# One VectorE instruction for mask and row maximum, a power on GpSimd for a root, and a reordered start, in an attention and feed-forward kernel

## The chip, the cores and the metric

The kernel runs on one core of one Trainium2 chip. Such a core has TensorE (PE; its weight loads are listed apart as PEld), VectorE (DVE), ScalarE (ACT), GpSimd (POOL) and a queue (SP) that issues DMAs between the chip's main memory and SBUF. TensorE writes its products into PSUM. The metric is the device time of one execution in microseconds, as a median over runs. Beside it stands the span of one profiled execution, from its first to its last instruction.

## The reference

One transformer layer in fp32, for x of shape 2 x 1024 x 512, with 16 heads of 32 and a hidden width of 2048:

```python
qkv = einsum('bsd,ed->bse', x, w_qkv) + b_qkv
scores = einsum('bhqd,bhkd->bhqk', q, k) / sqrt(32)
attn = softmax(scores + causal)          # causal: -inf above the diagonal
y = einsum('bsd,ed->bse', attn @ v, w_out) + b_out
x = layernorm(x + y)                     # (x - mean) / sqrt(var + 1e-5)
h = relu(einsum('bsd,hd->bsh', x, sign(up_weight)) * up_scale)
x = layernorm(x + einsum('bsh,dh->bsd', h, sign(down_weight)) * down_scale * output_scale)
```

## The kernel before

**Order.** The kernel does not issue instructions in the order of its loops. Every instruction or small group is given to a planner as a task: the engines that may run it with a cost for each (in microseconds), a due time called place, and the buffers that it reads, writes and updates. `Plan.schedule` then lists the tasks engine by engine: of those whose inputs would be ready by the planner's own clock, the one with the smallest place goes first. The order so found is fixed in the program; on the chip each engine runs its queue in that order and waits on semaphores. A changed cost or place can therefore move instructions anywhere.

**Attention.** The heads are taken in 8 chunks of four heads: 4 chunks for each batch element, in a row. A chunk needs its keys and queries for 1024 tokens (`product`, L549: fp32 matmuls of 128x512, four to a result), split into a high and a low part (ScalarE and VectorE for keys, L626 and L631; VectorE and GpSimd for queries, L570, L609 and L614) and copied by 32 small DMAs per part into "stacks" (`stack`; all DMAs are issued on L505), from which scores are computed at the faster fp32r rate. It also needs values (`values_of`, L586). The projection of the next chunk goes on while the present one attends: a chunk lasts `STEP = 36` units of place, keys and queries are due by `MID` of it (0.55), values from there to `HI` (1.0).

For each block of 128 query tokens, i = 0 to 7, and each head, only the keys up to that block count, so that N = 128 (i + 1) columns. Heads are grouped: four to a score tile for i below 2, two for i = 2 and 3, one above. `scores` does for one such group: the score matmuls into a PSUM pair, of which there are two (L789, or L770 in the first half of the first chunk, from unsplit keys and queries); the mask added to the diagonal block (L805); the row maximum of all its heads in one instruction, negated (L815); for each head the exponential with the maximum as bias and the row sum as a second output (L821); one reciprocal (L832); for each head the scaling of the row on GpSimd (L838). `transposes` turns the rows by TensorE (L859) and copies them out of PSUM (L487 on ScalarE, L489 on VectorE). `values` multiplies with the values (L888), at times for two query blocks together (those in `TOGETHER` are held back for the next), and VectorE adds the bias into atT (L908).

**Output projection and first normalisation.** In the last chunk of a batch element, `output` loads the rows of x, adds b_out on GpSimd (L944), multiplies by w_out (L950), adds (L961) and takes mean and variance (L965, L969). When all eight blocks are done, `normalise` takes the root of eight variances at once on ScalarE (L979), the reciprocal on VectorE (L983), and scales the eight blocks on VectorE (L988).

**Feed-forward.** Four blocks of 512 tokens. `turn` transposes the rows and splits them (L1013, L1020, L1025). For each of 16 hidden slices: eight matmuls (L1062), ReLU on ScalarE into hf (L1073), a split (L1079, L1084), eight matmuls into four PSUM banks pd (L1099). At the end of a block, for each of its four row tiles: scaling by output_scale and down_scale (L1113), the residual (L1123), statistics (L1129, L1134), root (L1139), reciprocal (L1145), scaling (L1150) and the store.

**Start.** `first_half` warms TensorE with 24 transposes (L703), loads the first weights on ScalarE's queue and the first 512 tokens of xT on SP's, four DMAs, computes keys and then queries of those tokens (the scheduler interleaves them), and starts attention with them. `hold` keeps the DMAs of the next tokens and of the value weights behind the landing of the first piece of xT by a one-column copy (L694).

Of the kernel before, what the change touches and what calls it, by code (L numbers as in the profile page):

```python
# [18 lines left out]
P = 128  # L19
EPS = 1e-5  # L20

MASKED = -3.0e38


# [5 lines left out]
LAST = [0, 1, 2, 7, 6, 5, 4, 3]  # L30
HURRY = 6.0

LAG = 6.0

MID, HI = 0.55, 1.0

# [238 lines left out]
def kernel(  # L275
# [26 lines left out]
    NFC = F // P  # L302
    TB = 512
    TPB = TB // P
    NG = F // TB
# [10 lines left out]

    mask = const.tile([P, P], F32, tag="mask", name="mask")
    nc.gpsimd.memset(mask, 0.0)
    nc.gpsimd.affine_select(
        out=mask,  # L320
        in_=mask,
        compare_op=ALU.is_ge,
# [5 lines left out]
    epst = const.tile([P, 1], F32, tag="eps", name="epst")  # L328
    nc.gpsimd.memset(epst, EPS)
    bqk = const.tile([P, b_qkvP.shape[1]], F32, tag="bqk", name="bqk")  # L330
    nc.gpsimd.dma_start(bqk, b_qkvP)
# [30 lines left out]
    def place_for(stack, name, n, kind=F32, side="left"):  # L362
# [14 lines left out]

    a_pr, a_pt = place_for(left, "probs", 4 * 2 * TB), place_for(left, "probsT", 8 * 2 * TB)

# [23 lines left out]
        "raw": [None],  # L403
        "hf": [None] * 4,
        "hh": [None] * 6,
# [14 lines left out]
    def reopen(cls):  # L420

        if cls == "raw" or cls == "xt" and homes["xt"][0] is None:
            right.close()
            xt = place_for(right, "xt0", 2 * NC * TB, F32R, "right")
            homes["xt"][:1] = views(xt, (2, NC, TB), F32R)
            raw = place_for(right, "raw", NC * TB, side="right")
            homes["raw"] = views(raw, (NC, TB))
        elif cls == "pd":
            wide.close()
            narrow = wide.enter_context(tc.tile_pool(name="narrow", bufs=1, space=PSUM))  # L430
            homes["pd"] = [
                narrow.tile([P, TB], F32, tag=f"pd{k}", name=f"pd{k}") for k in range(4)
            ]
        else:
            left.close()
            xt = place_for(left, "xt1", 2 * NC * TB, F32R)
            homes["xt"][1:] = views(xt, (2, NC, TB), F32R)
            homes["hf"] = views(place_for(left, "hf", 4 * TB), (TB,))
            hid = place_for(left, "hid", 12 * TB, F32R)
            homes["hh"] = views(hid, (TB,), F32R)[:6]  # L440
            homes["hr"] = views(hid, (TB,), F32R)[6:]

    def of(t):
# [8 lines left out]
    rings = {  # L452
        "pr": (a_pr, 4 * 2 * TB // P), "pt": (a_pt, 8 * 2 * TB // P)
    }
# [125 lines left out]
    def values_of(b, e, v, t0, place):  # L580

        xt, w, ps = inputs[b], weights[b, e], new("f")
        for t in range(4):
            for c in range(NC):
                def fn(_, t=t, c=c):
                    nc.tensor.matmul(  # L586
                        of(ps)[:, t, :],
                        lhsT=of(xt)[:, c, t0 + t * P : t0 + (t + 1) * P],
                        rhs=of(w)[:, c, 2, :],
                        start=(c == 0),  # L590
                        stop=(c == NC - 1),
                    )

                plan.task(
                    {"PE": (0.218, 0.218)}, fn, place(1), [xt[c, t0], w[2]], updates=[ps[0]],
                    count=2, label="ps_v",
                )

        plan.task(
            copy(TB),  # L600
            lambda g: copied(g, of(v)[:, t0 // P : t0 // P + 4, :], of(ps)),
            place(0) - FAST, [ps[0]], [v[t0]], label="v",
        )
# [94 lines left out]
    def first_half():  # L698
# [9 lines left out]
        for c, z in ((0, 1), (1, NC)):  # L708
# [9 lines left out]
            )  # L718
        load_x(0, -100, [0])
        xt = inputs[0]  # L720
        load_w(0, 0, -95, [0], act_queue)
# [8 lines left out]
        rows = lambda n: of(kq)[:, n * TB : (n + 1) * TB]  # L730
        for n in (1, 0):
            ps = product(0, 0, n, 0, lambda units: -50)
            with_bias(0, 0, n, lambda n=n: rows(n), [kq[n]], ps, -50)
        values_of(0, 0, v, 0, lambda units=0: -1)
        plain[0, 0] = kq, v

    def second_half():
# [3 lines left out]
        place = pace(-10, 6, 16 * 3)  # L741
        split(hl, 0, lambda: of(kq)[:, TB : 2 * TB], [kq[1]], -20)
        stack(st, 1, hl, 0, 0, TB, lambda: -20)
# [17 lines left out]
    def scores(b, e, i, heads, at):  # L761
# [3 lines left out]
        if (b, e) in plain and i < NQ // 2:  # L765
            kq = plain[b, e][0]

            def fn(_):
# [9 lines left out]
            plan.task(  # L778
                {"PE": (0.002 + N / 485,) * 2}, fn, at - EAGER, [kq[0], kq[1]], updates=[sc[0]],
                count=2 * G, label="sc4",  # L780
            )
        else:
            st = made[b, e][0]
            for j, u in enumerate(heads):
                for k0 in range(0, N, TB):
# [15 lines left out]
                    )  # L801
        sc3 = lambda: of(sc).rearrange("p (g w) -> p g w", g=G)
        plan.task(
            dve(0.163 + 0.134 * G),
            lambda _: nc.vector.tensor_tensor(  # L805
                sc3()[:, :, ts(i, P)],
                sc3()[:, :, ts(i, P)],
                mask[:, None, :].to_broadcast([P, G, P]),
                ALU.add,
            ),  # L810
            at, updates=[sc[0]], label="mask",
        )
        plan.task(
            dve(0.15 + 1.046 * N * G / 1000),
            lambda _: nc.vector.tensor_reduce(of(nm)[:, :G], sc3()[:, :, :N], AX.X, ALU.max, negate=True),  # L815
            at, [sc[0]], [nm[0]], label="max",
        )
        for j in range(G):
            plan.task(
                {"ACT": (0.355 + 0.838 * N / 1000, 0.46 + 0.838 * N / 1000)},  # L820
                lambda _, j=j: nc.scalar.activation(  # L821
                    of(pr)[:, j * N : (j + 1) * N],
                    of(sc)[:, j * W : j * W + N],
                    AF.Exp,
                    bias=of(nm)[:, j : j + 1],
                    accum_out=of(sums)[:, j : j + 1],
                ),
                at, [sc[0], nm[0]], [pr[j], sums[0]], label="exp",
            )
# [108 lines left out]
    def output(b, i, place):  # L938

        xb, st, a, py = new("xb"), new("st6"), atT[b, i], new("f")  # L940
        y = x1[b]
        dma(place(), lambda: of(xb), lambda: x[ts(b * NQ + i, P), :], 256, writes=[xb[0]])
        plan.task(
# [29 lines left out]
    def normalise(b, at):  # L973

        y, m = x1[b], mv[b]
        rs = lambda: of(m)[:, :, 2]
        plan.task(
            {"ACT": (2.8, 2.0)},
            lambda _: nc.scalar.activation(rs(), of(m)[:, :, 1], AF.Sqrt, bias=epst),  # L979
            at, [m[0]], [m[1]], label="sqrt",  # L980
        )
        plan.task(
            dve(0.16), lambda _: nc.vector.reciprocal(rs(), rs()), at, updates=[m[1]], label="rs"  # L983
        )
# [58 lines left out]
    def feed_forward(up, dn, dsc, base):  # L1043
        UNIT = 2.0

        def block(tb):
# [61 lines left out]
            for t in range(TPB):  # L1108
# [10 lines left out]
                if not final:  # L1119
# [28 lines left out]
                plan.task(  # L1148
                    {**dve(0.546), **pool(0.69)} if final and t + 1 < TPB else dve(0.546),
                    lambda e, m=m, y=y: engine[e].tensor_scalar(  # L1150
                        of(y), of(y), of(m)[:, 0:1], of(m)[:, 2:3], ALU.subtract, ALU.mult
# [14 lines left out]
    for at, (b, e) in enumerate(chunks):  # L1166
# [7 lines left out]
        for i in tiles:  # L1174
            begin[i] = past
            attend(b, e, i, past, i in TOGETHER and not (at == 0 and i < NQ // 2))
            past += i + 1
# [102 lines left out]
```

## Time and profile before

| | |
|---|---|
| median of three runs | 770.89 us (770.79 to 771.13) |
| the profiled execution: time, span | 772.01 us, 770.2 us |
| TensorE clock granted | 0.997 |
| busy in the span: PE, PEld, DVE, ACT, POOL | 752.4, 571.3, 519.6, 379.4, 257.1 us |
| busy of those before 517 us (attention) | 507.5, 375.9, 400.3, 318.9, 238.6 us |
| mask (L805) and maximum (L815), busy | 62.3 and 180.2 us, 178 instructions each |

An entry such as `L815 DVE TENSOR_REDUCE small<-d` names the line of the kernel, the engine, the operation, and the buffers written and read. The profile's views used here are the page of totals, a table by stretches of time (busy PE, PEld, DVE, ACT, POOL with instruction counts in brackets, then the clock, the DMA engines' share and GB/s), the list of who waited for whom (total us, times, longest), and the timeline (start, duration, instruction, and in square brackets the idle time before it and what ended it). Matmuls are pipelined and their ends are modelled, so that a PE shown busy need not be at full rate.

### The profile page before, as it was taken

How to read it: one execution, taken by the hardware profiler on the slowest of the kernel's cores; microseconds unless marked ns; L12 is line 12 of the kernel's file. 1: busy time of each engine (PE TensorE's matmuls, PEld its weight loads, DVE VectorE, ACT ScalarE, POOL GpSimd, SP SyncE). 2: the span in 40 equal slices, each digit the busy share in tenths (PEclk: the TensorE clock that was granted, in tenths of full speed). 3: DMA queues.
4: the chain of work that ended last, by engine and by line, in shares of the span. 5: the costliest groups of instructions: out<-in, count | busy, mean ns of one | idle time of the engine just before them, and what ended most of it. 6: DMA issues, size and time to landing. Idle time of an engine off the chain costs nothing.

```text
span 770.2 us, 15411 instructions
## 1 busy us (share of the span) xinstructions
PE 752.4 (98%) x5864; PEld 571.3 (74%) x5864; DVE 519.6 (67%) x1087; ACT 379.4 (49%) x841; POOL 257.1 (33%) x325
## 2 busy tenths in 40 slices
PE   8999999999999999899999999999999999999995
PEld 4668769778766775686876887758777887878884
DVE  1658898688787677878778889946336337335535
ACT  1426766776754556577756777744222222222210
POOL 2315455463446443544544644530002002002002
PEclk9999999999999999999999999999999999999998
DMA  6467556058151523532614514433001001000101
GB/s 182 107 156 157 142 111 138 14 116 223 34 124 46 120 69 69 126 82 56 139 27 101 120 57 138 137 110 110 1 0 56 1 0 56 1 0 1 55 0 55
DMA packets 38089, 62.35 MB, mean 81 GB/s; under 512 B 6016, under 2 KB 18304, under 8 KB 38016
## 3 DMA queue, kind: packets, MB, share of 16 engines
q1 hardware_dynamic: 36912, 60.85, 30.8%
q8 instruction: 46, 0.75, 0.4%
q10 hardware_dynamic: 1072, 0.52, 0.2%
q14 instruction: 27, 0.22, 0.1%
q0 software_dynamic: 32, 0.01, 0.0%
HBM read 24.66 MB, written 4.19 MB: 37 GB/s over the span
## 4 chain that ended last, share of the span: by engine, by line
PE 51%; DVE 5%; SPq 1%; ACT 1%; issue 1%; DMA 1%; POOL 0%; POOLq 0%; DVEq 0%; ACTq 0%
PE s L1062 14%; PE pd L1099 14%; PE s L859 6%; PE s L888 4%; PE d L789 4%; PE s L549 3%; PE s L950 3%; PE s L586 2%; SPq L505 1%; DVE small L1129 1%; PE s L1013 1%; DVE x L988 1%; DVE atT L1113 1%; DMA stacks<-wqkv 1%; DVE atT L1150 0%
## 5 line engine op out<-in xcount | busy, mean ns | idle before, releaser
L838 POOL TENSOR_SCALAR probs<-probs,small 128x128 f32<-128x128 f32 (+7 forms) x256 | 188.9, 747 | 243.2 <-DVE small L832 216.2
L821 ACT ACTIVATE probs<-d,small 128x128 f32<-128x128 f32 (+7 forms) x256 | 189.2, 747 | 73.5 <-DVE small L815 37.5
L815 DVE TENSOR_REDUCE small<-d 128x1 f32<-128x768 f32 (+9 forms) x178 | 180.2, 1016 | 3.0
L859 PE MATMUL s<-ident,probs 128*128 128x128 f32 x1152 | 162.7, 273 | 3.1 <-POOL probs L838 1.9
L859 PEld LDWEIGHTS s<-ident,probs 128*128 128x128 f32 x1152 | 134.0, 140 | 42.1 <-issue 20.0
L487 ACT COPY probsT<-s 128x512 f32<-128x512 f32 (+3 forms) x193 | 95.3, 523 | 92.3 <-PE s L859 82.4
L1099 PE MATMUL pd<-stacks,hid 128*128 128x512 f32 x512 | 133.4, 399 | 0.5 <-DVE hid L1079 0.5
L1062 PE MATMUL s<-xt,stacks 128*128 128x512 f32 x512 | 133.2, 400 | 0.0
L549 PE MATMUL s<-xT,wqkv 128*128 128x512 f32 x256 | 128.4, 598 | 1.0 <-DMA wqkv<-in_w_qkvT 1.0
L789 PE MATMUL d<-stacks 128*128 128x512 f32 (+2 forms) x368 | 123.7, 426 | 2.8 <-DMA stacks<-wqkv 1.4
L1073 ACT ACTIVATE hf<-s,ups 128x512 f32<-128x512 f32 x64 | 44.0, 687 | 160.2 <-PE s L1062 158.7
L1099 PEld LDWEIGHTS pd<-stacks,hid 128*128 128x128 f32 x512 | 94.3, 188 | 24.1 <-DVE hid L1079 1.4
L1062 PEld LDWEIGHTS s<-xt,stacks 128*128 128x128 f32 x512 | 94.3, 188 | 23.5 <-issue 1.0
L1079 DVE CAST hid<-hf 128x512 fp32r<-128x512 f32 x64 | 27.7, 435 | 121.6 <-ACT hf L1073 121.5
L489 DVE COPY probsT<-s 128x512 f32<-128x512 f32 (+3 forms) x152 | 86.9, 587 | 17.3 <-PE s L859 11.7
L789 PEld LDWEIGHTS d<-stacks 128*128 128x128 f32 x368 | 59.6, 190 | 39.1 <-issue 24.5
L805 DVE TENSOR_TENSOR d<-d,mask 128x128 f32<-128x128 f32 (+2 forms) x178 | 62.3, 352 | 29.3 <-PE d L789 23.4
L888 PEld LDWEIGHTS s<-probsT,v 128*32 128x32 f32 x2304 | 60.4, 110 | 18.7 <-issue 5.4
L586 PE MATMUL s<-wqkv,xT 128*128 128x128 f32 x512 | 72.9, 276 | 0.0
L888 PE MATMUL s<-probsT,v 128*32 128x128 f32 x2304 | 71.6, 274 | 0.2 <-DVE probsT L489 0.2
L586 PEld LDWEIGHTS s<-wqkv,xT 128*128 128x128 f32 x512 | 66.3, 192 | 6.4 <-issue 5.4
L950 PE MATMUL s<-wout,atT 128*128 128x512 f32 x128 | 64.1, 597 | 0.1
(65 smaller groups left out, 486.9 us busy)
## 6 DMA issues: line engine op xcount, KB each, us to landing
stacks<-wqkv SPq DMA_DIRECT2D x224, 128.0 KB, 2.4
wqkv<-in_w_qkvT SPq DMA_DIRECT2D x22, 256.0 KB, 3.5
xT<-in_xT SPq DMA_DIRECT2D x16, 256.0 KB, 5.3
rows<-in_x SPq DMA_DIRECT2D x16, 256.0 KB, 3.0
raw<-in_up_wT SPq DMA_DIRECT2D x4, 1024.0 KB, 5.0
out<-atT SPq DMA_DIRECT2D x16, 256.0 KB, 2.0
stacks<-wqkv SPq DMA_DIRECT2D x48, 64.0 KB, 2.0
raw<-in_down_wT SPq DMA_DIRECT2D x2, 1024.0 KB, 5.8
```

The lines of the kernel that those rows point to most:

```text
L487: nc.scalar.copy(dst, src)
L549: nc.tensor.matmul(of(ps).rearrange("p a b -> p (a b)"), lhsT=of(w)[:, c, n, :], rhs=of(xt)[:, c, t0 : t0 + TB], start=(c == 0), stop=(c = ...
L586: nc.tensor.matmul(of(ps)[:, t, :], lhsT=of(xt)[:, c, t0 + t * P : t0 + (t + 1) * P], rhs=of(w)[:, c, 2, :], start=(c == 0), stop=(c == NC ...
L789: nc.tensor.matmul(of(sc)[:, j * W + k0 : j * W + k1], lhsT=of(st)[:, 0, u, ts(i, P)], rhs=of(st)[:, 1, u, k0:k1], start=True, stop=True,)
L815: lambda _: nc.vector.tensor_reduce(of(nm)[:, :G], sc3()[:, :, :N], AX.X, ALU.max, negate=True),
L821: lambda _, j=j: nc.scalar.activation(of(pr)[:, j * N : (j + 1) * N], of(sc)[:, j * W : j * W + N], AF.Exp, bias=of(nm)[:, j : j + 1], acc ...
L838: lambda _, j=j: nc.gpsimd.tensor_scalar(of(pr)[:, j * N : (j + 1) * N], of(pr)[:, j * N : (j + 1) * N], of(sums)[:, j : j + 1], 1.0, ALU. ...
L859: lambda _, k=k, c=c, tp=tp: nc.tensor.transpose(of(tp)[:, k, :], of(pr)[:, c], ident),
L888: nc.tensor.matmul(of(to)[ts(u, HD), n, :], lhsT=of(v)[:, k, ts(u, HD)], rhs=of(pt)[:, ts(c + k, P)], start=(k == i), stop=(k == 0),)
L950: lambda _, c=c: nc.tensor.matmul(bank(py), lhsT=of(a)[:, c, :], rhs=of(wout)[:, c, :], start=(c == 0), stop=(c == NC - 1),),
L1062: lambda _, f=f, c=c, n=n, pu=pu: nc.tensor.matmul(of(pu), lhsT=of(up)[:, f // TPB, c, ts(f % TPB, P)], rhs=of(xt)[:, n, c, :], start=(c = ...
L1099: lambda _, f=f, t=t, n=n, h=h: nc.tensor.matmul(of(pds[t]), lhsT=of(h)[:, ts(t, P)], rhs=of(dn)[:, f // 4, f % 4, :], start=(f == 0 and n ...
```

## The change

- **Mask and maximum.** For each head, one two-operand VectorE instruction reads the N score columns and the last N columns of a mask that is now 1024 wide (zeros, with the triangle in the last 128), writes -(score + mask) back over the scores, and gives their minimum, with the largest float as the start value, as a second output. That minimum is the negated maximum. The exponential takes scale -1, and depends on its own head's instruction alone.
- **First normalisation.** The root on ScalarE and the reciprocal on VectorE give way to two GpSimd instructions on eight columns: add epsilon, then raise to the power -0.5.
- **First tokens.** The first 512 tokens of xT are loaded as 256 (four DMAs) and 256 (one DMA), and their keys and queries computed and copied out by halves, in that order; what reads them depends on the half that it needs.
- **Next keys.** `MID` is 0.45 in place of 0.55.
- **Room for the mask.** The ring of transposed rows has 60 blocks of 128 in place of 64, and hf has three buffers in place of four.
- **Small parts.** The planner places the loads of rows in `output` after the last stack DMA known by then. In the last block of the feed-forward the final scaling (L1150) is for VectorE alone; before, GpSimd might take it. The last query block of a chunk is never held back.

```diff
-MID, HI = 0.55, 1.0
+MID, HI = 0.45, 1.0
...
-    mask = const.tile([P, P], F32, tag="mask", name="mask")
+    mask = const.tile([P, S], F32, tag="mask", name="mask")
     nc.gpsimd.memset(mask, 0.0)
     nc.gpsimd.affine_select(
-        out=mask,
-        in_=mask,
+        out=mask[:, S - P :],
+        in_=mask[:, S - P :],
...
-    a_pr, a_pt = place_for(left, "probs", 4 * 2 * TB), place_for(left, "probsT", 8 * 2 * TB)
+    a_pr, a_pt = place_for(left, "probs", 4 * 2 * TB), place_for(left, "probsT", PTB * P)
...
-        "hf": [None] * 4,
+        "hf": [None] * 3,
...
-        load_x(0, -100, [0])
-        xt = inputs[0]
+        xt = inputs[0] = new("xT")
+        for t0, pieces in ((0, NC), (HB, 1)):
+            for c in range(0, NC, NC // pieces):
+                z = c + NC // pieces
+                dma(
+                    -100,
+                    lambda c=c, z=z, t0=t0: of(xt)[:, c:z, t0 : t0 + HB],
...
-        for n in (1, 0):
-            ps = product(0, 0, n, 0, lambda units: -50)
-            with_bias(0, 0, n, lambda n=n: rows(n), [kq[n]], ps, -50)
+        for t0 in (0, HB):
+            for n in (1, 0):
+                ps = new("f")
+                for c in range(NC):
...
+                        nc.tensor.matmul(
+                            bank(ps)[:, :HB],
+                            lhsT=of(w)[:, c, n, :],
+                            rhs=of(xt)[:, c, t0 : t0 + HB],
...
-        plan.task(
-            dve(0.163 + 0.134 * G),
-            lambda _: nc.vector.tensor_tensor(
-                sc3()[:, :, ts(i, P)],
-                sc3()[:, :, ts(i, P)],
-                mask[:, None, :].to_broadcast([P, G, P]),
-                ALU.add,
-            ),
-            at, updates=[sc[0]], label="mask",
-        )
-        plan.task(
-            dve(0.15 + 1.046 * N * G / 1000),
-            lambda _: nc.vector.tensor_reduce(of(nm)[:, :G], sc3()[:, :, :N], AX.X, ALU.max, negate=True),
-            at, [sc[0]], [nm[0]], label="max",
-        )
+        for j in range(G):
+            some = lambda j=j: of(sc)[:, j * W : j * W + N]
+            plan.task(
+                dve(0.17 + 1.046 * N / 1000),
+                lambda _, j=j, some=some: nc.vector.tensor_tensor_reduce(
+                    some(),
+                    some(),
+                    mask[:, S - N :],
+                    scale=-1.0,
+                    scalar=LARGEST,
+                    op0=ALU.add,
+                    op1=ALU.min,
+                    accum_out=of(nm)[:, j : j + 1],
+                ),
+                at, [sc[0]], [sc[1, j], nm[j]], label="max",
+            )
...
                     bias=of(nm)[:, j : j + 1],
+                    scale=-1.0,
                     accum_out=of(sums)[:, j : j + 1],
                 ),
-                at, [sc[0], nm[0]], [pr[j], sums[0]], label="exp",
+                at, [sc[1, j], nm[j]], [pr[j], sums[0]], label="exp",
...
-        dma(place(), lambda: of(xb), lambda: x[ts(b * NQ + i, P), :], 256, writes=[xb[0]])
+        dma(
+            place(), lambda: of(xb), lambda: x[ts(b * NQ + i, P), :], 256, writes=[xb[0]],
+            after=[latest["stack"]],
+        )
...
         plan.task(
-            {"ACT": (2.8, 2.0)},
-            lambda _: nc.scalar.activation(rs(), of(m)[:, :, 1], AF.Sqrt, bias=epst),
-            at, [m[0]], [m[1]], label="sqrt",
+            pool(0.3),
+            lambda _: nc.gpsimd.tensor_scalar(
+                rs(), of(m)[:, :, 1], EPS, 1.0, ALU.add, ALU.mult
+            ),
+            at, [m[0]], [m[1]], label="eps",
         )
         plan.task(
-            dve(0.16), lambda _: nc.vector.reciprocal(rs(), rs()), at, updates=[m[1]], label="rs"
+            pool(1.2),
+            lambda _: nc.gpsimd.tensor_tensor(
+                rs(), rs(), half.to_broadcast([P, NQ]), ALU.pow
+            ),
+            at, updates=[m[1]], label="rs",
         )
...
-                    {**dve(0.546), **pool(0.69)} if final and t + 1 < TPB else dve(0.546),
-                    lambda e, m=m, y=y: engine[e].tensor_scalar(
+                    dve(0.546),
+                    lambda _, m=m, y=y: nc.vector.tensor_scalar(
...
-            attend(b, e, i, past, i in TOGETHER and not (at == 0 and i < NQ // 2))
+            apart = i == tiles[-1] or at == 0 and i < NQ // 2
+            attend(b, e, i, past, i in TOGETHER and not apart)
```

## The prediction

> **What bounds the kernel now.** I read the page's busy times first, then the table of stretches of 20 us, then who the PE waited for, then the timeline around each hole.
>
> ```profile
> span 770.2 us, 15411 instructions
> ...
> PE 752.4 (98%) x5864; PEld 571.3 (74%) x5864; DVE 519.6 (67%) x1087; ACT 379.4 (49%) x841; POOL 257.1 (33%) x325
> ...
> 0.00:20.00 20.00, 16.59 (x60) 9.23 (x60) 3.74 (x14) 3.47 (x10) 5.11 (x16) 1.00 0.60 179
> ...
> 180.00:200.00 20.00, 18.45 (x245) 15.58 (x245) 16.22 (x34) 13.47 (x25) 8.10 (x8) 1.00 0.62 178
> ...
> 300.00:320.00 20.00, 17.70 (x139) 11.51 (x142) 18.73 (x41) 11.57 (x23) 7.08 (x8) 1.00 0.54 120
> ...
> 380.00:400.00 20.00, 18.58 (x239) 16.73 (x238) 14.09 (x28) 14.07 (x39) 7.86 (x12) 1.00 0.36 78
> ```
>
> In the stretches the numbers are PE, PEld, DVE, ACT, POOL busy. TensorE is the bound: it idles only 17.8 us (770.2 - 752.4): 3.4 in the first 20 us, 1.55, 2.30 and 1.42 in the three later stretches, 7.7 after its last matmul, 1.4 scattered. From 517 us on (feed-forward) it is packed. What the change can win lies in the start, three holes, the end, and waits too short to show as idle. The latter are in the waits of the weight loads:
>
> ```profile
> PEld d L789 <- ACT probs L821: 12.7, 37, 1.3
> PEld s L859 <- POOL probs L838: 11.4, 25, 2.0
> ```
>
> A score matmul waits until the exponential has freed its PSUM pair; a transpose waits for a normalised row. Both stand at the end of mask, maximum, exponential, scaling. TensorE feels part of these 24.1 us (62 waits), since it still drains what was issued: its own waits for the exponential are 1.4 us.
>
> **What the Trainium skill says.** "VectorE: DVE Perf Modes", Why PSUM operands drop a tier: an fp32 operand in PSUM holds VectorE to one element a cycle. The trace agrees: maxima of 1024 and 640 columns take 1221 and 819 ns, 1.05 ns an element and 0.15 fixed. The same page, Two Vector instructions with no wait between them: an operation that also gives out its accumulator is two instructions; the changed kernel's VectorE queue shows both, the before trace no VectorE one. "Vector Engine (DVE) Microarchitecture Reference", Points that are easy to get wrong: the two-tensor form with an accumulator runs at half speed when both sources are non-bf16 in SBUF. Here one is in PSUM; L631, of this mix but without an accumulator, shows no halving (741 ns for 512 columns). "GPSIMD Engine Reference", Key points: GpSimd shares its SBUF interfaces with VectorE, to the cost of two-port instructions there. The trace agrees:
>
> ```profile
> 306.65 0.55 DVE L988 TENSOR_SCALAR x<-x,small 128x512 f32<-128x512 f32 x1
> ...
> 310.79 3.65 DVE L988 TENSOR_SCALAR x<-x,small 128x512 f32<-128x512 f32 x4
> ```
>
> The first had POOL idle (0.55 us); the four stood beside POOL work and took 0.91 each.
>
> **The change, part by part.**
>
> *Mask and maximum.* Removed: L805 and L815, 62.3 + 180.2 = 242.5 us in 356 instructions. Added: 256 pairs, one per head and row tile. Columns: 8 chunks x 4 heads x 128 x (1+...+8) = 147,456, by 1.05 ns 155 us; fixed 0.15 (maximum) to 0.20 (L631), 45 us; the read-out by VectorE's smallest instructions (four in 0.33 us) 0.08, 20 us. Sum 220: VectorE gets 22 us back. Bounds: 40 us back (read-out free, 0.15 fixed), or, at half speed, 310 + 71 = 381, 139 us more. I take 220, as L631's mix is the nearest. More important is the delay to the exponential. One head of 1024 columns: mask start to maximum end was 1.54 us (190.70 to 192.24), now 1.02 x 1.05 + 0.2 + 0.1 = 1.38. Two heads of 384: 1.43 before both; now 0.7 for the first. Four of 256: 1.9; now 0.55. Taking 0.15 from each of the 62 waits gives 9.3 us of weight-load waiting; TensorE sees less than half. I book -3.5 (0 to -9).
>
> *Keys at 0.45.* One hole is keys' and queries' stacks landing late: at 389.03 a score matmul had waited 1.42 us for stacks<-wqkv. SP issued the last 18 of 32 stack DMAs from 368.48 to 386.24, each queued behind the landing of an earlier one. In the built order, summing TensorE work by the trace's intervals, the last key/query product stands 12.6 us ahead of that chunk in before, 15.1 in after: about the 2.5 needed. In the first batch it stands 15 to 17 ahead; 1 to 3 in before are early products of the chunk after. The values are spread up to and past each chunk's start. At 190.47 to 192.02 TensorE had neither values nor products left (next batch's xT still loading) and waited 1.55 for POOL's rows; in after 12 value products stand there. I book -1.4 and -1.5 (0 to -3 together; up to +3 if the later-freed xT delays the second batch's loads: these eight are queued on SP behind one more 256 KB rows load).
>
> *First normalisation.* On ACT two table loads of 1.28 and a root of 0.31 sat at 301.55 to 307.26 around a copy, and the exponential whose maximum was ready at 304.25 began at 307.28; then TensorE waited 0.45 for it. This goes. The eight L988 remain bunched ahead of the next fused instructions, and held two score tiles (0.94 and 0.91 of TensorE idle). The power is on GpSimd: no row of before has one. Lower bound: a short POOL instruction, 0.37 (128 columns); upper 5 us, an estimate of over ten times that[...]. Behind it on POOL stand a row scaling and a split, behind the first L988 on VectorE a bias, copies and the next maxima. I take 1 us: -1.0 of the 2.3 (to +3 at 5 us). The second normalisation lies in the packed feed-forward: nothing, covered by its matmuls until those tokens' transposes, some 60 us later (L988 near 528, L1013 of xT from 590).
>
> *Start.* Before: the first product ran 5.9 to 7.8, TensorE waited for query weights until 8.81, then 6 x 0.857 to 14.23, and 0.94 for the bias copies. Now two half products precede the same wait; the weights come on ACT's own queue, behind the same bytes: 8.7 again. Then 6 x 0.43, 0.6 bias, 0.5 scores, second halves 8 x 0.43: at 15.8 TensorE has done what before had done at 15.67. Of before's gaps until 32 us (six of about 0.2) about 0.8 close, as the first softmax starts 3 us earlier: -0.7 (+1 to -2). The mask's fill is 8 times wider (0.20 now; at POOL's 0.84 ns a column up to 0.95) and holds back the identity, warm-up and the bias load by 0.75: covered by the weights' wait; uncovered, it costs that. The extra half-width DMA is one SP issue of 0.45, in the shadow of the first loads.
>
> *End.* From 762.46 VectorE was continuous until its last instruction:
>
> ```profile
> 762.51 0.74 DVE L1113 SCALAR_TENSOR_TENSOR atT<-pd,osc,v 128x512 f32<-128x512 f32 x1
> ...
> 763.42 2.07 POOL L1150 TENSOR_SCALAR atT<-atT,small 128x512 f32<-128x512 f32 x1 [0.69 <-DVE small L1145]
> 763.83 0.90 DVE L1123 TENSOR_TENSOR atT<-atT,xT 128x512 f32<-128x512 f32 x1
> ...
> 766.30 0.55 DVE L1150 TENSOR_SCALAR atT<-atT,small 128x512 f32<-128x512 f32 x1
> ```
>
> Two final scalings move from POOL (2.07 each) to VectorE (0.52); in the built order the second falls after the last matmul, +0.52; the add at 763.83 had been slowed from 0.69 to 0.90 by POOL and gets 0.2 back; one add moves to POOL, off the end. +0.4 (0 to +0.7).
>
> *At nothing:* three buffers for four behind ReLU (one is used every 3.7 us, free after about 2), ring of 60 blocks for 64 (44 held plus two units of 7 fit either; a wrap may cost a short wait), the later-ordered rows loads (POOL waited 15 us for these with TensorE running). The condition on the last tile names no tile of TOGETHER.
>
> *Sum:* -3.5 - 2.9 - 1.0 - 0.7 + 0.4 = -7.7. A new order moves about 5000 TensorE instructions, and its own short waits can't be read from the trace: I give back 2, an estimate from holes of 1.4 to 2.3 that the old order left. -5.7: span 764.5. The profiled execution took 772.0, 1.1 above the median of 770.89 and 1.8 above its span; against the median 765.2.
>
> **Rivals.**
> *Forecast, 0.50:* half the short waits and most holes close: 762 to 768.5.
> *Short waits vanish too, 0.13:* the 62 waits were mostly felt, and the order is kept: 5 us more, 760. For: TensorE's busy time contains modelled ends. Against: only 1.4 of the 12.7 shows as its own wait.
> *Gain lost in the order, 0.27:* each hole was filled by earlier products, which then lack elsewhere; late xT or a slow power opens another. Then 768 to 777, most likely 770.5, that is unchanged. For: no work is removed from TensorE (same matmuls, 8 split in two). Against: the holes have distinct causes, and each is addressed.
> *VectorE becomes the bound, 0.10, slower:* the fused instruction runs at half speed. 139 us more on the 400 that VectorE has before 517 us gives 539; in its fullest stretch it reached 94% with TensorE losing 2.3 of 20, so 539/0.94 = 573, 56 later: 827. It decides from about 1.2 ns an element, where 147,456 x 1.2 + 66 fixed equals the 242.5 removed. For: no accumulator on VectorE in the trace. Against: L631.
>
> **How the numbers follow.** Measurement tells 0.2% (1.5 us). Faster: 0.50 + 0.13 + 0.06 of the third = 0.69; same 0.10; slower 0.11 + 0.10. Range 759.5 to 773 takes in the forecast, most of the second, two thirds of the third; the forecast's own is 762 to 768.5.
>
> **What would show it.** Fused rows near 1.3 us at 1024 columns with a read-out under 0.2; VectorE under 505 us in all; weight-load waits for exponentials and rows well under 24; no idle for stacks; no table load before the feed-forward; first scores near 12.2 (15.17 before); TensorE's last matmul at 754 to 759 and the end some 8.1 after it. Wrong if fused rows exceed 1.45, the power exceeds 3, or new holes over 1 us open where the second batch's xT arrives.

## The result and the profile after

The changed kernel takes 776.18 us (median of 6 runs, 775.27 to 776.88) beside 771.01 us for the kernel before (6 runs, 770.14 to 771.34): ratio 1.0068, 95% interval 1.0055 to 1.0081. It is 5.2 us slower, where 5.7 us faster was forecast. The page of the changed kernel:

```profile
span 774.1 us, 15524 instructions
...
PE 756.1 (98%) x5880; PEld 574.9 (74%) x5880; DVE 492.4 (64%) x1258; ACT 368.9 (48%) x823; POOL 259.1 (33%) x329
```

VectorE has 27.2 us less to do (519.6 before). TensorE, with the same products, shows 3.7 us *more* busy time and the same idle (18.0 us for 17.8). The ends of matmuls are modelled, so a matmul whose successor comes a little late may look longer: a loss that shows as busy time is likely to be many short delays, with few holes. The stretches, first of the changed kernel (columns as in the prediction: PE, PEld, DVE, ACT, POOL busy, then clock, DMA share, GB/s):

```profile
0.00:20.00 20.00, 17.12 (x81) 12.85 (x82) 5.17 (x27) 5.66 (x19) 6.76 (x19) 1.00 0.54 161
...
140.00:160.00 20.00, 19.32 (x186) 14.21 (x185) 15.69 (x50) 14.60 (x47) 10.15 (x18) 1.00 0.05 15
180.00:200.00 20.00, 20.00 (x276) 18.85 (x276) 14.70 (x43) 12.67 (x31) 10.01 (x11) 1.00 0.68 167
200.00:220.00 20.00, 18.91 (x168) 12.50 (x167) 15.91 (x48) 13.81 (x39) 10.01 (x18) 1.00 0.31 93
300.00:320.00 20.00, 19.77 (x147) 13.15 (x146) 17.71 (x42) 11.44 (x24) 11.33 (x13) 1.00 0.50 110
340.00:360.00 20.00, 19.31 (x172) 13.15 (x171) 15.59 (x47) 14.28 (x40) 10.73 (x19) 1.00 0.05 14
```

And three of the kernel before:

```profile
140.00:160.00 20.00, 20.00 (x177) 13.56 (x176) 15.57 (x30) 14.86 (x42) 7.79 (x14) 1.00 0.14 31
...
200.00:220.00 20.00, 20.00 (x178) 13.74 (x176) 15.78 (x33) 15.15 (x48) 10.15 (x18) 1.00 0.05 11
...
340.00:360.00 20.00, 20.00 (x224) 14.02 (x223) 17.14 (x38) 14.30 (x39) 10.10 (x18) 1.00 0.08 21
```

The old holes did close: 180 to 200 went from 18.45 to 20.00, 300 to 320 from 17.70 to 19.77. In their place TensorE idles 0.7 to 1.1 us in the stretches 140, 200 and 340, each the first 20 us after a chunk begins (chunks begin at 137.16, 193.55 and 333.74: the first score matmuls of 128 columns).

The whole loss is in attention. The first feed-forward matmul comes at 520.77 us, 4.1 later than before (516.68); from there to the end both need the same (253.3 and 253.5). The weight loads' waits that carried the prediction:

```profile
PEld d L839 <- ACT probs L872: 14.9, 39, 1.0
...
PEld s L940 <- ACT probs L872: 7.6, 10, 0.8
...
PEld s L911 <- POOL probs L890: 3.8, 10, 0.7
```

The transposes wait less for scaled rows (11.4 to 3.8). The score matmuls wait more for exponentials (12.7 to 14.9), and so do the products with the values (3.8 to 7.6): there the exponentials do not come earlier, but later.

And the fused instruction itself, in groups by shape, from 30 to 510 us (busy, mean ns; then idle before it):

```profile
L857 DVE CUSTOM_DVE_ANT_0 d<-d,mask 128x1024 f32<-128x1024 f32 x32 | 38.9, 1232 | 1.3 <-PE d L839 0.9
...
L857 DVE DVE_READ_ACCUMULATOR2_ANT small<- 128x1 f32 x240 | 33.9, 141 | 0.0
...
L857 DVE CUSTOM_DVE_ANT_0 d<-d,mask 128x256 f32<-128x256 f32 x28 | 12.0, 430 | 6.7 <-ACT probs L872 3.7 <-PE d L839 2.7
```

It runs at full speed (1.05 ns an element again). But look at the last field of the 256-column row: VectorE stood still 3.7 us in front of these instructions for *ScalarE's exponentials*. No mask or maximum of the kernel before waits for ScalarE in its built program. Here is one such place, the second row tile of the chunk that begins at 137.16, in the timeline (start, duration, instruction, in brackets the idle time and what ended it):

```profile
141.44 0.43 DVE L857 CUSTOM_DVE_ANT_0 d<-d,mask 128x256 f32<-128x256 f32 x1 [0.34 <-PE d L839]
...
141.79 0.69 DVE L494 COPY probsT<-s 128x512 f32<-128x512 f32 x1
...
142.40 0.42 DVE L857 CUSTOM_DVE_ANT_0 d<-d,mask 128x256 f32<-128x256 f32 x1
...
142.91 0.47 ACT L872 ACTIVATE probs<-d,small 128x256 f32<-128x256 f32 x1
...
143.51 0.43 DVE L857 CUSTOM_DVE_ANT_0 d<-d,mask 128x256 f32<-128x256 f32 x1 [0.60 <-ACT probs L872]
...
144.03 0.43 DVE L857 CUSTOM_DVE_ANT_0 d<-d,mask 128x256 f32<-128x256 f32 x1
144.38 0.14 DVE L857 DVE_READ_ACCUMULATOR2_ANT small<- 128x1 f32 x1
...
144.62 0.47 ACT L872 ACTIVATE probs<-d,small 128x256 f32<-128x256 f32 x1 [1.14 <-DVE small L857]
...
145.08 1.06 ACT L492 COPY probsT<-s 128x512 f32<-128x512 f32 x2
...
145.71 1.12 PE L554 MATMUL s<-xT,wqkv 128*128 128x512 f32 x2 [0.53 <-ACT probsT L492]
...
146.76 1.69 PEld L940 LDWEIGHTS s<-probsT,v 128*32 128x32 f32 x64 [0.76 <-ACT probs L872]
```

Four heads of 256 columns. Between the first and the second, a copy. The first exponential starts at 142.91; the third head starts only when it is over, 143.51. The second exponential, whose maximum had been read out by 142.88, starts only at 144.62, after the *fourth* head's read-out. Behind it on ScalarE stand two copies of transposed probabilities, and behind these TensorE: 0.53 us idle, and a weight load at 146.76 that then waits 0.76 us for an exponential. From the first fused instruction to the last read-out this tile took 3.08 us. In the kernel before, mask and maximum took 1.95 for five of the seven such tiles, and 2.48 for two in which other work came between mask and maximum.

### The profile page after: what moved, and what is told of

The parts are those of the page before. It is cut to its first block, busy times and chain, and to the rows that moved or that the text cites. A ratio compares the mean times of both kernels' runs of the same rounds, so it can differ in the third digit from the quotient of the medians.

```text
span 774.1 us, 15524 instructions
## 1 busy us (share of the span) xinstructions
PE 756.1 (98%) x5880; PEld 574.9 (74%) x5880; DVE 492.4 (64%) x1258; ACT 368.9 (48%) x823; POOL 259.1 (33%) x329
## 4 chain that ended last, share of the span: by engine, by line
PE 86%; DVE 9%; ACT 3%; issue 1%; POOL 1%; ACTq 0%; POOLq 0%; DVEq 0%
PE s L1122 14%; PE pd L1159 14%; PE s L911 13%; PE s L554 12%; PE d L839 9%; PE s L940 9%; PE s L1005 6%; PE s L591 6%; DVE d L857 3%; ACT probs L872 2%; DVE probsT L494 1%; PE s L754 1%; ACT probsT L492 1%; DVE small L1189 1%; PE s L1073 1%
## 5 line engine op out<-in xcount | busy, mean ns | idle before, releaser
L857 DVE CUSTOM_DVE_ANT_0 d<-d,mask 128x128 f32<-128x128 f32 (+7 forms) x256 | 194.0, 765 | 31.5 <-PE d L839 19.9
L911 PE MATMUL s<-ident,probs 128*128 128x128 f32 x1152 | 164.4, 273 | 1.7 <-DVE probsT L494 0.8
L492 ACT COPY probsT<-s 128x512 f32<-128x512 f32 (+3 forms) x184 | 90.9, 528 | 129.4 <-PE s L911 114.8
L554 PE MATMUL s<-xT,wqkv 128*128 128x512 f32 x240 | 119.0, 599 | 2.1 <-ACT probsT L492 1.6
L839 PE MATMUL d<-stacks 128*128 128x512 f32 (+2 forms) x368 | 117.0, 416 | 1.1 <-ACT probs L872 0.4
L494 DVE COPY probsT<-s 128x512 f32<-128x512 f32 (+3 forms) x161 | 91.1, 582 | 27.4 <-PE s L911 24.4
L554 PEld LDWEIGHTS s<-xT,wqkv 128*128 128x128 f32 x240 | 39.2, 190 | 25.2 <-issue 20.6
```

Source lines behind the costliest of these rows:

```text
L494: nc.vector.tensor_copy(dst, src)
L554: nc.tensor.matmul(of(ps).rearrange("p a b -> p (a b)"), lhsT=of(w)[:, c, n, :], rhs=of(xt)[:, c, t0 : t0 + TB], start=(c == 0), stop=(c = ...
L839: nc.tensor.matmul(of(sc)[:, j * W + k0 : j * W + k1], lhsT=of(st)[:, 0, u, ts(i, P)], rhs=of(st)[:, 1, u, k0:k1], start=True, stop=True,)
L857: lambda _, j=j, some=some: nc.vector.tensor_tensor_reduce(some(), some(), mask[:, S - N :], scale=-1.0, scalar=LARGEST, op0=ALU.add, op1= ...
L911: lambda _, k=k, c=c, tp=tp: nc.tensor.transpose(of(tp)[:, k, :], of(pr)[:, c], ident),
```

## The experiments

**1. Which part loses.** Two theories at first: the earlier keys (A), or the fused instruction in tiles of several heads (B).

e1, the changed kernel:
```diff
-MID, HI = 0.45, 1.0
+MID, HI = 0.55, 1.0
```


> The changed kernel with the keys' and queries' products spread over 0.55 of a chunk again instead of 0.45; everything else as changed. Theory A (the early keys are the loss: their products no longer reach into the next chunk's first small tiles, where the changed kernel loses 1 to 2 us after each chunk start): 769 to 772 us, back at the kernel before or under it. Theory B (one fused instruction per head makes the small, grouped tiles slower, four heads in turn with a read-out each): stays at 775 to 777. Theory C (only a reshuffled order, no single cause): 772 to 775.

e2, the kernel before:
```diff
-MID, HI = 0.55, 1.0
+MID, HI = 0.45, 1.0
```


> The kernel before with the keys' and queries' products at 0.45 of a chunk, nothing else. Theory A: 774 to 777 us, the whole loss from this edit alone. Theory B: 769.5 to 771.5, no loss. Theory C: 771 to 774.

e3, the changed kernel:
```diff
-        for j in range(G):
-            plan.task(dve(0.17 + 1.046 * N / 1000), ... tensor_tensor_reduce(...) ...)
+        plan.task(dve(0.163 + 0.134 * G), ... tensor_tensor(... mask[:, None, S - P :] ... ALU.add) ...)
+        plan.task(dve(0.15 + 1.046 * N * G / 1000), ... tensor_reduce(... ALU.max, negate=True) ...)
```


> The changed kernel with mask and maximum again as two VectorE instructions per tile (all heads of a group together), everything else as changed. Theory A: 776 to 779 us, as the fused instruction does not hurt and its gain is given up. Theory B: 769 to 772, as the grouped tiles are back at the old pace. Theory C: 773 to 777.

e4, the kernel before:
```diff
+PTB = 60                                   # ring of transposed blocks, 64 before
-        "hf": [None] * 4,
+        "hf": [None] * 3,
-    mask = const.tile([P, P], F32, ...)
+    mask = const.tile([P, S], F32, ...)
-        mask (tensor_tensor) and max (tensor_reduce), one each per tile
+        tensor_tensor_reduce, one per head, as in the changed kernel
```


> The kernel before with the fused mask and maximum alone, with the wide mask and the room it needs (60 blocks in the ring of transposed probabilities instead of 64, three buffers behind ReLU instead of four). Theory A: 766 to 770 us, the short waits for exponentials and rows shrink with no loss elsewhere. Theory B: 773 to 777. Theory C: 769 to 773.

| | us | ratio to before, 95% |
|---|---|---|
| e1 changed, keys at 0.55 | 783.23 | 1.0151 (1.0138 to 1.0165) |
| e2 before, keys at 0.45 | 768.30 | 0.9959 (0.9946 to 0.9971) |
| e3 changed, two instructions | 768.40 | 0.9960 (0.9947 to 0.9972) |
| e4 before, fused | 780.71 | 1.0119 (1.0103 to 1.0134) |

(before beside them: 771.72.) e1 lies outside all three forecasts, and theory A falls twice over: earlier keys win 3.4 us alone and 7.0 us on top of the fused instruction. The fused instruction costs 7.8 us in the changed kernel and 9.0 in the kernel before, more than I had expected of any theory. (The kernel before took 771.0 us beside the changed kernel and 771.4 to 771.7 beside the experiments, so that differences from the 776.2 of the changed kernel are uncertain by some 0.7 us.) e2 and e3 differ by all the other edits (start, first normalisation, room, rows' loads, end): 0.1 us together, which their intervals of about 1 us each can't tell from none.

The waits of e4 suggest also why the early keys matter more with the fused instruction: at 0.55 the stacks are late more often (3.3 us in five waits, where the kernel before had one of 1.4):

```profile
PE d L791 <- ACT probs L824: 5.8, 11, 1.4
PE d L791 <- DMA stacks<-wqkv: 3.3, 5, 1.1
```

**2. Where the fused instruction loses, and by what.** Four edits of the changed kernel. e5 and e6 choose by group:
```diff
+        fused = G == 1          # e5;  e6: fused = G > 1
+        if fused:  one fused instruction per head
+        else:      mask, then maximum, for the whole tile
```


> The changed kernel, fused instruction kept only for tiles with one head at a time (row tiles 4 to 7, 640 to 1024 columns); tiles of two or four heads get the old mask and maximum back. Theory B (the loss sits in the grouped tiles just after each chunk start): 766 to 769 us, at or under the 768.4 of the run with two instructions everywhere. Theory D (the fused instruction hurts wherever it stands, for example because the order planned with its cost is poorer): 772 to 776.

> The reverse: fused only for tiles of two or four heads, the old two instructions for single heads. Theory B: 774 to 778 us. Theory D: 770 to 774, between the two.

e7 makes the fused instructions of a tile one task of the planner:
```diff
-        for j in range(G):
-            plan.task(dve(0.17 + 1.046 * N / 1000), one head, at, [sc[0]], [sc[1, j], nm[j]], label="max")
+        plan.task(dve((0.17 + 1.046 * N / 1000) * G), all heads, at, [sc[0]],
+                  [x for j in range(G) for x in (sc[1, j], nm[j])], label="max")
```


> The changed kernel with the fused instructions of a tile planned as one piece of work, so that no copy comes between the heads and none of them is queued behind an exponential of its own tile (in the changed kernel's VectorE queue 8 of the 256 wait for ScalarE, 7 of these the third head of a four-head tile of 256 columns). Theory B1 (the splitting of the group makes the loss): 769 to 772 us. Theory B2 (the loss is the length of head-by-head work itself, or of a read-out the planner doesn't know): 775 to 778.

e8 changes a cost only:
```diff
-                dve(0.17 + 1.046 * N / 1000),
+                dve(0.27 + 1.046 * N / 1000),
```


> The changed kernel with the planner told 0.27 us fixed instead of 0.17 for each fused instruction (measured pitch 0.39 at 128 and 0.53 at 256 columns, that is 0.26 fixed), only the order can change. Theory B2 (the planner orders by a cost that leaves out the read-out): 769 to 772 us. Theory B1: 774 to 777, since the group stays split.

| | us | ratio to before, 95% |
|---|---|---|
| e5 fused for single heads only | 764.75 | 0.9914 (0.9901 to 0.9928) |
| e6 fused for groups only | 775.29 | 1.0049 (1.0037 to 1.0062) |
| e7 heads of a tile together | 766.22 | 0.9938 (0.9925 to 0.9950) |
| e8 read-out in the price | 768.89 | 0.9964 (0.9952 to 0.9977) |

(before: 771.40.) For single heads the fused instruction *wins* 3.65 us (e3 to e5), so that e5 lies below even theory B's forecast. For groups it loses: 6.9 us (e3 to e6), 11.4 (e5 to the changed kernel). Yet it need not: with the same instructions kept together, e7, 10.0 of the 11.4 are gone. VectorE's timeline of e7, a tile of four heads of 256 columns:

```profile
139.65 0.43 DVE L855 CUSTOM_DVE_ANT_0 d<-d,mask 128x256 f32<-128x256 f32 x1 [0.34 <-PE d L839]
140.00 0.14 DVE L855 DVE_READ_ACCUMULATOR2_ANT small<- 128x1 f32 x1
140.17 0.43 DVE L855 CUSTOM_DVE_ANT_0 d<-d,mask 128x256 f32<-128x256 f32 x1
...
140.70 0.43 DVE L855 CUSTOM_DVE_ANT_0 d<-d,mask 128x256 f32<-128x256 f32 x1
...
141.22 0.43 DVE L855 CUSTOM_DVE_ANT_0 d<-d,mask 128x256 f32<-128x256 f32 x1
141.57 0.14 DVE L855 DVE_READ_ACCUMULATOR2_ANT small<- 128x1 f32 x1
```

2.06 us from start to last read-out (1.95 with two instructions). So neither the fused instruction's length (theory B2's first half) nor its read-out is the loss, but the order. e7 comes out even below what theory B1 had forecast. e8, by its time, is close to the forecast of theory B2 that the planner's price is the fault. But the price acts through the order too: with 0.10 us more on each, the planner lists the tasks in another order. Of the seven tiles with four heads of 256 columns, five are whole in the program built for e8, none in that of the changed kernel; theory B1's forecast for e8, that the group stays split, was wrong. And a true price isn't needed: e7 keeps the old one and wins more.

The stretches of e5 that answer to 140 and 340 above:

```profile
140.00:160.00 20.00, 20.00 (x181) 14.21 (x180) 16.91 (x39) 14.81 (x42) 9.81 (x18) 1.00 0.07 18
...
340.00:360.00 20.00, 20.00 (x162) 12.94 (x161) 16.02 (x41) 13.61 (x33) 8.93 (x13) 1.00 0.31 67
```

**3. The other edits, on the version e5.**

e9, the start whole again, with the dependences on halves taken out as well:
```diff
-        for t0, pieces in ((0, NC), (HB, 1)):      # loads of the first tokens in halves
-        ...
-        for t0 in (0, HB):                          # products in halves
+        load_x(0, -100, [0])
+        for n in (1, 0):
+            ps = product(0, 0, n, 0, lambda units: -50)
```


> The version with the fused instruction for single heads only (764.75 us), with the first tokens loaded and multiplied whole again instead of in halves. If the halves win the 0.7 us that the prediction booked: 765.4 us. If they win nothing (the first transposes of the changed kernel came at 32.1 us, of the kernel before at 32.0): 764.5 to 765.0.

e10, the root on ScalarE again:
```diff
-        plan.task(pool(0.3), ... tensor_scalar(EPS, 1.0, ALU.add, ALU.mult) ...)
-        plan.task(pool(1.2), ... tensor_tensor(rs(), rs(), half, ALU.pow) ...)
+        plan.task({"ACT": (2.8, 2.0)}, ... activation(AF.Sqrt, bias=epst) ...)
+        plan.task(dve(0.16), ... reciprocal ...)
```


> The version with the fused instruction for single heads only (764.75 us), with the root of the first normalisation on ScalarE again (two table loads) and the reciprocal on VectorE. If the power on GpSimd wins the 1.0 us booked: 765.8 us; all of the hole: 767. If it wins nothing because the earlier keys already fill that hole: 764.5 to 765.0.

e11, the price of e8:
```diff
-                dve(0.17 + 1.046 * N / 1000),
+                dve(0.27 + 1.046 * N / 1000),
```


> The version with the fused instruction for single heads only (764.75 us), with the read-out in the planner's cost (0.27 us fixed for 0.17). If a true price helps only where groups can be split: 764.3 to 765.2, no change. If it helps for single heads too: 762 to 764. If it only shuffles: 765.5 to 767.

e12:
```diff
-MID, HI = 0.45, 1.0
+MID, HI = 0.40, 1.0
```


> The version with the fused instruction for single heads only (764.75 us), with keys and queries over 0.40 of a chunk instead of 0.45. If earlier is still better: 763 to 764.3. If 0.45 already leaves the stacks no wait (none shows in the changed kernel): 764.5 to 765.5; if products packed closer crowd out other work: 766 to 768.

Beside 771.71 for before: e9 768.45 (ratio 0.9961, 0.9945 to 0.9976), e10 764.49 (0.9907, 0.9894 to 0.9921), e11 764.81 (0.9909, 0.9895 to 0.9924), e12 767.91 (0.9951, 0.9936 to 0.9967). So the root on GpSimd wins nothing once the keys are early, and the price changes nothing where no group can be split. Keys at 0.40 lose 3.2 us, as forecast for products that crowd out other work. The loss has no single place: beside e5, 1.2 us are lost by the end of chunk 2, 1.5 in chunk 4 and 1.3 after chunk 8 has begun, while the sixth and seventh chunks are as long as in e5 (54.7 and 54.8 us).

e9 is a surprise: the halves are worth 3.7 us there, outside both forecasts. But not at the start. Up to 40 us TensorE has done as much in e9 as in e5. (e9's expectation sets a matmul at 32.1 us beside a weight load at 32.0; matmul beside matmul, the changed kernel's first transposes came at 32.10 us and those of the kernel before at 32.39.) The loss is at 51 to 56 us (the PE's timeline, then stretches of 1 us with the clock third from the end):

```profile
52.33 0.71 PE L796 MATMUL d<-stacks 128*128 128x512 f32 x2 [1.35 <-ACT probs L847]
```

```profile
51.00:52.00 1.00, 0.00 (x0) 0.00 (x0) 1.00 (x4) 0.61 (x1) 0.00 (x0) 1.00 0.28 73
52.00:53.00 1.00, 0.67 (x2) 0.30 (x2) 0.24 (x3) 1.00 (x4) 0.43 (x1) 0.78 1.08 317
53.00:54.00 1.00, 0.62 (x4) 0.58 (x4) 0.92 (x3) 1.00 (x3) 0.36 (x1) 0.50 0.54 165
...
55.00:56.00 1.00, 1.00 (x3) 0.52 (x2) 1.00 (x3) 1.00 (x4) 0.52 (x1) 0.51 0.83 184
56.00:57.00 1.00, 1.00 (x5) 0.51 (x3) 0.31 (x3) 0.87 (x4) 0.87 (x2) 1.00 1.01 221
```

A score matmul waited 1.35 us for an exponential, a transpose 0.38 after it, and from 52.6 to 56.0 TensorE ran at half its clock: 1.35 + 0.38 + half of 3.4 is 3.4 us. "TensorE: Matmul & The Clock Gate" of the Trainium skill, Part 1: The HAM clock gate, describes this: activity is judged in free-running windows of about 3.4 us, and after an idle one the clock is halved. The trace agrees on the half and on the length; but here, of the 3.4 us before the clock fell, TensorE was idle only for 1.35, while the kernel before kept full clock around its wait of 1.55 us at 190:

```profile
190.00:192.00 2.00, 0.47 (x2) 0.04 (x1) 1.97 (x4) 2.00 (x5) 1.01 (x1) 1.00 0.76 242
```

So e9 shows an order in the middle of the first chunk that fell badly, and not the start's own worth.

**4. What in the split group costs.** Keeping the heads together (e7) took away two things: the copies between them, and a later head's wait for an exponential of its own tile. (e7's expectation has the third head wait in all seven tiles; in the built program it is the third in five, in one tile the second and the fourth, and in one none.) Two edits of the changed kernel.

e13, every exponential planned behind all heads' maxima:
```diff
-                at, [sc[1, j], nm[j]], [pr[j], sums[0]], label="exp",
+                at, [x for h in range(G) for x in (sc[1, h], nm[h])], [pr[j], sums[0]], label="exp",
```


> The changed kernel with one more dependence in the plan: an exponential is planned only after the fused instructions of all heads of its tile. Copies and reciprocals may still come between the heads (in the built program 8 of the 9 tiles of 256 columns are still split, by 14 instructions, against 9 by 17), but no fused instruction is queued behind an exponential of its own tile (0 against 8). If that wait is the loss: 766 to 769 us. If the work in between is the loss: 774 to 777. If both have a share: 770 to 773.

e14, the single task of e7 for row tile 1 only:
```diff
+        if i == 1:  all heads in one task, as in e7
+        else:       head by head, as in the changed kernel
```


> The changed kernel with the heads kept together only in the tiles of four heads and 256 columns, the second row tile of a chunk; the other grouped tiles planned head by head as changed. If the loss is this tile's (it is split in every chunk, the others seldom): 766 to 768.5 us, the 766.2 of all heads together or little over. If the tiles of 384 and 512 columns carry a share: 769 to 773.

(The counts of split tiles in e13's expectation are off: of the seven tiles with four heads of 256 columns, six are split by 10 instructions in e13, seven by 13 in the changed kernel. The counts of waits stand.)

e13: 768.09 (0.9967, 0.9956 to 0.9979; three of its ten runs took 770.2 to 771.0); e14: 769.05 (0.9973, 0.9962 to 0.9984); before 771.53. Without the wait 8.1 us are won, with the tiles still split, as forecast for the case that the wait is the loss:

```profile
334.03 0.43 DVE L857 CUSTOM_DVE_ANT_0 d<-d,mask 128x256 f32<-128x256 f32 x1 [0.34 <-PE d L839]
...
334.38 0.69 DVE L494 COPY probsT<-s 128x512 f32<-128x512 f32 x1
...
334.99 0.42 DVE L857 CUSTOM_DVE_ANT_0 d<-d,mask 128x256 f32<-128x256 f32 x1
...
335.50 0.43 DVE L857 CUSTOM_DVE_ANT_0 d<-d,mask 128x256 f32<-128x256 f32 x1
...
336.02 0.43 DVE L857 CUSTOM_DVE_ANT_0 d<-d,mask 128x256 f32<-128x256 f32 x1
```

The copy stands between the heads as in the changed kernel, but the third follows the second (335.50) without a wait. Such a tile takes 2.06 to 2.52 us here, where six of the seven took 3.08 or 3.31 in the changed kernel. And the score matmuls' weight loads wait for exponentials 7.8 us in all, where it was 14.9:

```profile
PEld d L839 <- ACT probs L872: 7.8, 25, 1.0
```

Keeping only this one row tile together wins 7.1; e7, with the other groups together too, is 2.8 us faster still. The orders side by side (fused instructions that wait for ScalarE as counted in the built program's VectorE queue; chunk lengths between the first 128-column score matmuls of chunks 6, 7 and 8):

| | us | waiting, in all | of these with 256 columns | 6th, 7th chunk, us |
|---|---|---|---|---|
| e1 | 783.2 | 17 | 10 | 57.2, 57.2 |
| e4 | 780.7 | 16 | 10 | 56.6, 58.8 |
| changed kernel | 776.2 | 8 | 7 | 56.3, 56.3 |
| e6 | 775.3 | 9 | 7 | 56.6, 55.7 |
| e14 | 769.1 | 1 | 0 | 54.8, 54.8 |
| e8 | 768.9 | 8 | 2 | 55.2, 55.5 |
| e13 | 768.1 | 0 | 0 | 54.8, 54.8 |
| e7 | 766.2 | 0 | 0 | 54.8, 54.8 |
| e5 | 764.8 | 0 | 0 | 54.8, 54.9 |

The fifth column shows the price in two chunks, 1.5 us each between e5 and the changed kernel. From the start of chunk 2 to the feed-forward the changed kernel takes 439.9 us and e5 428.4, so that the 11.4 us between the two lie in the seven chunks that have such tiles, though unevenly (0.4 to 2.9 each). e8 tells which of the waits count: it has as many as the changed kernel, but only two with 256 columns and five in tiles of two heads, and it is 7.3 us faster.

Why a head with columns of its own waits for another head's exponential can be read in part from the built programs. In the six that have such waits (the changed kernel, e1, e4, e6, e8, e14), the 59 fused instructions that wait for ScalarE are exactly those that stand behind an exponential of their own score tile in the order of the program. Each waits for such an exponential, and that one reads other columns. So the waits go as if the score tile were one thing. Which rule in the building of the program sets them, no run isolates. What else stays open: every edit also changes the order of everything else, so the differences between the five lowest rows, up to 4.3 us, are not assigned to single causes.

## Why the prediction was wrong

**What bounds the kernel, and the holes:** right. TensorE sets the time, the holes at 190, 310 and 389 went, and no matmul of the changed kernel waits for the stacks any more. Keys at 0.45 were booked at -2.9; alone they measure -3.4 (e2).

**Mask and maximum, its cost:** the stream was as worked out (1232 ns for 1024 columns). The read-out was taken as 0.08 us and takes 0.141; the sum of the rows is 230.2 us (194.0 and 36.2) for 220 forecast and 242.5 before. "VectorE: DVE Perf Modes" of the Trainium skill, Two Vector instructions with no wait between them, has such an operation as two instructions, and the trace shows the pair for every one. No half speed: that rival is out. (The bound of 40 us back, for a free read-out and 0.15 fixed, was mis-summed: 155 + 38 is 193, and 242.5 less that is 49.)

**Mask and maximum, the delay to the exponential: here the prediction failed.** It said "Four of 256: 1.9; now 0.55" and took 0.15 us off each of 62 waits. 0.55 is the *first* head's delay. What releases the score pair and the reciprocal is the last one. Two tasks for four heads had become four, between which a planner may put other work, as it could before, and into whose middle an exponential may come, as it could not before. Measured: 3.08 us to the last head. What is queued behind a waiting instruction was asked of the old waits, not of the new ones; in the built order a fused instruction waits for ScalarE 8 times, and a mask or maximum of before never. The term of -3.5 was +7.8 in the changed kernel (e3 to the changed kernel). These are two parts: -3.65 where a tile has one head, where nothing can be split and the same reasoning held (e3 to e5), and +11.4 where it has several (e5 to the changed kernel).

**The allowance for a new order, +2:** it was the only term that could have held such a loss, but it was an estimate from the old holes, and no wait of the new order stood behind it.

**First normalisation, -1.0:** the power took 1.67 us, not 1, within the bounds; VectorE waited 0.57 for it:

```profile
307.21 1.68 POOL L1040 TENSOR_TENSOR small<-small,half 128x8 f32<-128x8 f32 x1
...
308.93 1.46 DVE L1048 TENSOR_SCALAR x<-x,small 128x512 f32<-128x512 f32 x3 [0.57 <-POOL small L1040]
```

The two table loads at 301.55 and 305.98 are gone. Yet the root on ScalarE costs no time with the early keys (e10), so nothing was won; what hides it there is not shown.

**Start, -0.7:** the first scores came at 11.42 us (12.2 forecast, 15.17 before), but at the first transposes, with the same products done, only 0.3 us were left of the lead (32.10 us, 32.39 before). The wide mask delays TensorE's warm-up to 2.21 us (1.45 before), as said.

**End, +0.4:** nothing. TensorE's last matmul ends at 766.36 and the kernel at 774.1, 7.7 later, as before. VectorE's last scaling did come later, 4.7 us after that matmul for 4.4 before, but the kernel's end did not:

```profile
763.63 2.73 PE L1159 MATMUL pd<-stacks,hid 128*128 128x512 f32 x11
```

```profile
769.86 0.52 DVE L1210 TENSOR_SCALAR atT<-atT,small 128x512 f32<-128x512 f32 x1
...
770.51 0.55 DVE L1210 TENSOR_SCALAR atT<-atT,small 128x512 f32<-128x512 f32 x1
```

**The rivals:** the time fell into the third's interval (768 to 777), "gain lost in the order", but not by its mechanism: the filled holes took nothing from elsewhere, as e2 shows. What was lost came from a wait that no rival named. Most signs named for the forecast didn't give it away either: fused rows at 1.23 us, VectorE at 492 us, no wait for stacks and a power of 1.7 us all fell on its side; only TensorE's last matmul, at 766 us for 754 to 759, did not. The forecast of 765.2 describes e5, the same change without fusing groups, within 0.5 us. In part that is luck: single heads and keys won about what was booked (-3.65 and -3.4), but -1.0 for the root measured nothing, and the +2 for a new order has no counterpart there.

## What to carry to other kernels

When one instruction for a whole tile is replaced by one per part, price the *last* part, not the first, and read in the built order what comes between the parts and what each of them waits for. A consumer that is released by the first part can end up inside the group and hold back a later one. Keep such parts one task for a scheduler, or fuse only where there is one part: here that turned a loss of 5.2 us into a gain of 5.2 (e7) or 6.7 (e5).

## What the runs showed of the hardware beyond expectation

A VectorE instruction with an accumulator is followed by a read-out of 141 ns, which partly overlaps: fused instructions of 128 columns (300 ns) in a row start every 0.39 us, those of 256 (430 ns) every 0.52. A power of 128x8 on GpSimd took 1.66 and 1.68 us, eight columns costing more than a scaling of 1024 (1.12). And in e9 one wait of 1.35 us was followed by 3.4 us at half clock, which cost more than the wait; what makes the clock fall after one such wait and not after another, these runs don't show.
